# Moving the drives of 8 of 32 scans to ScalarE and TensorE, and the inner projection out of the convolution

## The chip, the cores and the metric

The kernel runs on one core of a Trainium2 chip. Five engines work side by side, each through its own queue of instructions in order: PE (TensorE, matrix multiplications and transposes), DVE (VectorE), ACT (ScalarE), POOL (GpSimd) and SP (SyncE, which here only issues DMAs). They meet through semaphores. SBUF is the memory that all of them read, PSUM the one that PE writes[...]. The metric is the device time of one execution in microseconds (us), from the first to the last instruction. Everything is fp32.

## The reference

Two layers on x of shape (2, 256, 256, 128), each as x = x + layer(group_norm(x)). The first is an attention along one axis of the image; the change doesn't touch it. The second is a selective scan over the 65,536 pixels of each image, with 256 inner channels and 16 states for each:

```python
xz = x @ in_proj_w.T
xi, z = jnp.split(xz, 2, axis=-1)
xi = silu(depthwise_conv_3x3(xi, conv_w) + conv_b)       # 256 channels
x_dbl = einsum('bdl,cd->bcl', xs, x_proj_w[0])           # xs is xi, L = H * W
dts, Bs, Cs = x_dbl[:, :8], x_dbl[:, 8:24], x_dbl[:, 24:]
delta = softplus(einsum('brl,dr->bdl', dts, dt_w[0]) + dt_b)
# for every channel d and state n, along the pixels t:
#   h = exp(delta * A) * h + (delta * xs) * Bs ;  y = sum over n of h * Cs
y = y + Ds * xs
y = layer_norm(y) * ln_g + ln_b
y = y * silu(z)
return y @ out_proj_w.T
```

(Names are shortened and the scan is put in two lines; the computation is that of the reference.)

## The kernel before

The program has two stages. The first computes group statistics and the attention, and leaves the first layer's result in DRAM as `x1`. The second walks over the two images in 128 steps of four rows, T = 1024 pixels each (`R`, `T`, `steps`).

A step has 32 scan units. A unit is a group of 32 channels with four states each, so that 32 x 4 = 128 partitions hold one recurrence each, and time runs along the free dimension. Two halves of 128 channels, four groups `m` of states and four groups `q` of channels make the 32. For a unit:

- `fetch` (line 1003) loads what it needs by DMA: `delta` and `du` = delta x xs, each row repeated for the four states, and the rows of B (`bb`) and C (`cc`), each repeated for the 32 channels. Each of these is 512 KB in SBUF. `delta_r` has five buffers, `du_r` three pairs, `bb` and `cc` two each.
- `decay` (1034): ACT takes exp(delta x A) into the PSUM tile `da`, of which there are two, for odd and even units.
- `drive` (1042): POOL multiplies du by B for two units at once into `hb`.
- `scan` (1055): DVE's tensor_tensor_scan runs h = da x h + hb from the stored state, and leaves h in `da`, or in `hb` where POOL will read it.
- `remember` (1062): ACT copies the last column of h to the state.
- `product` (1067) on DVE, or `products` (1077) for a pair on POOL: h x C into `yc`. POOL takes five pairs and a single unit of each step (`POOLED`, `SINGLE`, lines 638 and 639), DVE the other 21.
- `add_up` (1100): PE adds the four states of each channel with the 128x32 matrix `sel`. Four units write 32 rows each of the PSUM tile `y`; `y_out` copies it.

Beside the scans of step k run the pieces that prepare later steps (`project`, line 675) and finish earlier ones (`finish`, line 862). Preparation turns the image rows so that channels lie on partitions, normalises them (`xn`, with a column of padding at either side), and computes the inner projection and the 3x3 convolution in one: nine accumulated matmuls of 128x512 with weights `w_tap`, the projection's weights times one tap each (`conv`, 731). Then come the gate's projection (`gate`), two SiLUs, the projection to delta, B and C (`states`, `size`), softplus, and `times` (828), where POOL multiplies delta by xs. Results go through DRAM, so that `fetch` can repeat them. Finishing a row takes the layer norm over channels, the gate (`gated`, on DVE) and the output projection.

The order of instructions on PE, ACT, DVE and POOL is that in which the code writes them (`tc.manual_schedule`); the order on SP is the scheduler's. The loop at the end (line 1134) goes through time slots t, one for each unit, and writes for each slot the fetch for six slots ahead, the drive for three ahead, the decay for one ahead, the scan, and then whatever pieces stand in that slot's list. `at(t, piece)` puts them there; preparation starts 84 slots before the first scan of its step (`base - 12`, with base = 32 k - 72).

Stretches of lines in the text above are those of the kernel before. A function's place in the queue follows from this loop alone:

```python
if 0 <= t + 3 < end and t % 2:
    drive(t + 3)
if 0 <= t + 1 < end:
    decay(t + 1)
if 0 <= t < end:
    scan(t)
```

Of the kernel before, what the change touches and what calls it, by code (L numbers as in the profile page):

```python
# [15 lines left out]
P = 128  # L16
# [5 lines left out]
def attn_then_ssm_kernel(  # L22
# [113 lines left out]
    w_tap = const.tile([P, NH, 9, P], F32, name="w_tap")  # L136
# [17 lines left out]
    )  # L154
    with tc.tile_pool(name="prep", bufs=1) as prep, tc.tile_pool(
# [4 lines left out]
        cw = prep.tile([P, NH, 9], F32, name="cw")  # L160
        nc.sync.dma_start(out=cw, in_=conv_w.rearrange("(h p) o i j -> p h (o i j)", p=P))
# [41 lines left out]
        for h in range(NH):  # L203
            for tap in range(9):
                wt = prep2.tile([P, P], F32, name="wt")
                nc.vector.tensor_scalar(wt, inp[:, h, :], cw[:, h, tap : tap + 1], None, ALU.mult)
                transposed(w_tap[:, h, tap, :], wt, P)
            transposed(w_z[:, h, :], inp[:, NH + h, :], P)
            for i, by in enumerate((lng_c, lnb_c)):
                transposed(w_out[:, i, h, :], outp[:, h * P : (h + 1) * P], P)  # L210
                nc.vector.tensor_scalar(
                    w_out[:, i, h, :], w_out[:, i, h, :], by[:, h : h + 1], None, ALU.mult
                )
            transposed(w_xp[:, h, :], xpw[:, h * P : (h + 1) * P], 64)
            transposed(w_dt[:, h, :], dtw[:, h, :], P)
            nc.vector.tensor_scalar(d_diag[:, h, :], ident, ds_c[:, h : h + 1], None, ALU.mult)
# [415 lines left out]
    RB = TB // W  # L632
# [5 lines left out]
    POOLED = (6, 14, 22, 26, 30)  # L638
    SINGLE = 11
    s1 = ctx.enter_context(tc.tile_pool(name="s1", bufs=1))  # L640
    s2 = ctx.enter_context(tc.tile_pool(name="s2", bufs=2))
    s3 = ctx.enter_context(tc.tile_pool(name="s3", bufs=3))
    s4 = ctx.enter_context(tc.tile_pool(name="s4", bufs=4))
# [10 lines left out]
    slots = {}  # L654
    between = {}

    def at(t, piece, *args, pe=False):

        slots.setdefault(t, ([], []))[pe].append((piece, args))

    xn = s1.tile([P, R + 2, WP], F32, name="xn")
    nc.gpsimd.memset(xn, 0.0)
    given = {}
# [6 lines left out]
    for i, piece in enumerate(pieces):  # L672
        at(i - 2, piece)

    def project(k):
# [3 lines left out]
        base = k * NU - 72  # L679
# [4 lines left out]
        def bank(shape, name):  # L684

            o["n"] = o.get("n", 0) + (k == 0)
            pool, tag = ((ps_p, "p"), (ps_f, "f"))[o["n"] % 2]
# [10 lines left out]
        def begin():  # L698
            if s == 0:
                if k > 0:  # L700
                    nc.gpsimd.memset(xn[:, 0, 1 : W + 1], 0.0)
# [7 lines left out]
            else:  # L709
                nc.scalar.copy(xn[:, 0:2, 1 : W + 1], xn[:, R : R + 2, 1 : W + 1])  # L710
            if n < R:
                nc.gpsimd.memset(xn[:, 2 + n, 1 : W + 1], 0.0)
# [9 lines left out]
        def normalise(to, m):  # L722
            nc.scalar.activation(
                xn[:, to : to + m, 1 : W + 1],
# [6 lines left out]
        def conv(h, i, taps):  # L731
            if taps[0] == 0:
                o["u"] = bank([P, RB, W], "u_ps")
            for tap in taps:
                dy, dx = divmod(tap, 3)
                nc.tensor.matmul(  # L736
                    o["u"],
                    w_tap[:, h, tap, :],
                    xn[:, i * RB + dy : i * RB + dy + RB, dx : dx + W],
                    start=(tap == 0),  # L740
                    stop=(tap == 8),
                )
# [11 lines left out]
        def silu_xs():  # L754
            nc.scalar.activation(o["xs"], o["xs"], AF.Silu)
            exp_and_ln()
            v["xs"] = dr.tile([NH, P, T], F32, name="xs_d")
            nc.sync.dma_start(out=v["xs"].rearrange("h p t -> p h t"), in_=o["xs"])

        def gate(h, i):  # L760
            o["z"] = bank([P, RB, W], "z_ps")
            nc.tensor.matmul(  # L762
                o["z"],
                w_z[:, h, :],
                xn[:, 1 + i * RB : 1 + (i + 1) * RB, 1 : W + 1],
# [4 lines left out]
        def gate_out(h, i):  # L770
            if (h, i) == (0, 0):
                o["sz"] = s1.tile([P, NH, T], F32, name="sz")
            nc.scalar.copy(  # L773
                o["sz"][:, h, i * TB : (i + 1) * TB], o["z"].rearrange("p r w -> p (r w)")
            )

        def silu_z():
            nc.scalar.activation(o["sz"], o["sz"], AF.Silu)
            exp_and_ln()
            v["sz"] = dr.tile([NH, P, T], F32, name="sz_d")  # L780
            nc.sync.dma_start(out=v["sz"].rearrange("h p t -> p h t"), in_=o["sz"])
# [12 lines left out]
        def states_out(i):  # L794
            if i == 0:
                v["bc"] = dr.tile([2 * NS, T], F32, name="bc_d")
                o["xd"] = s1.tile([64, T], F32, name="xd")
# [14 lines left out]
        def size_out(h, i):  # L812
            if (h, i) == (0, 0):
                o["delta"] = s1.tile([P, NH, T], F32, name="delta")
# [20 lines left out]
        at(base - 12, load)  # L835
        at(base, begin)
        for r in range(0, n, RB):
            t = base + r // RB
            at(t, turn, "raw", r, min(RB, n - r), pe=True)
            at(t + 1, normalise, 2 + r, min(RB, n - r))  # L840
        CY = NU // 4
        for c in range(4):
            h, i = divmod(c, NB)
            t = base + c * CY + 3
            for dt, taps in ((0, (0, 1, 2)), (1, (3, 4, 5)), (2, (6, 7)), (3, (8,))):
                at(t + dt, conv, h, i, taps, pe=True)
            at(t + 5, conv_out, h, i)
        for t, (h, i) in ((2, (0, 0)), (24, (0, 1)), (25, (1, 0)), (26, (1, 1))):
            at(base + t, gate, h, i, pe=True)
            at(base + t + 1, gate_out, h, i)  # L850
        at(base + 28, silu_z)
        at(base + 36, silu_xs)
        for t, i in ((40, 0), (41, 1)):
            at(base + t, states, i, pe=True)
            at(base + t + 1, states_out, i)
        for t, (h, i) in ((42, (0, 0)), (48, (1, 0)), (49, (0, 1)), (50, (1, 1))):
            at(base + t, size, h, i, pe=True)
            at(base + t + 1, size_out, h, i)
        at(base + 52, softplus)
        at(base + 55, times)  # L860

    def finish(k):

        b, s = steps[k]
        for r in range(R):
            if k + 1 < len(steps):
                a = (r + 1) * (NU // R)
            else:
                a = 4 + r * (NU // R // 2)
            finish_row(k, b, R * s + r, r * W, (k + 1) * NU + a)  # L870

    def finish_row(k, b, row, t0, a):
# [14 lines left out]
        def fetch():  # L887
# [9 lines left out]
        def turn():  # L897
# [11 lines left out]
        def stats():  # L909
            yn = o["yn"] = room(  # L910
                "yn", "delta", lambda t: t[:, :, 0:DI], [P, WT, DI], [P, NH, T], s1
            )
# [6 lines left out]
        def scales():  # L919
# [5 lines left out]
        def norm():  # L925
# [8 lines left out]
        def back():  # L934
# [9 lines left out]
        def gated():  # L944
            o["yg"] = room("yg", "xs", lambda t: t[:, :, 0:W], [P, NH, W], [P, NH, T], s2)
            nc.vector.tensor_tensor(o["yg"], o["yd"], o["szr"], ALU.mult)  # L946

        def mix():
# [13 lines left out]
        def leave():  # L962
# [14 lines left out]
        at(a, fetch)  # L977
        for i, piece in (
            (0, turn),
            (1, stats),  # L980
            (2, scales),
            (3, norm),
            (4, back),
            (7, mix),
            (8, leave),
        ):
            at(a + i, piece, pe=piece in (turn, back, mix))
        between[a + 5] = gated
# [3 lines left out]
    units = {}  # L992

    def unit(t):

        k, i = divmod(t, NU)
        h, i = divmod(i, NM)
        m, q = divmod(i, NQ)
        return k, h, m, q
# [3 lines left out]
    def fetch(t):  # L1003
        k, h, m, q = unit(t)
        v = given[k]
        if q == 0:

            for name, row in (("bb", m * SR), ("cc", NS + m * SR)):
# [197 lines left out]
```

## Time and profile before

| what | us |
|---|---|
| median of three runs | 15813.17 (15807.9 to 15815.29) |
| span of the profiled execution | 15811.9 |
| first scan starts, last scan ends, in that execution | 2631.2, 15772.6 |
| one scan on DVE, 128x1024 | 2.34 |
| one product on DVE | 1.22 |
| one drive or product of a pair on POOL, 128x2048 | 4.54 |
| one exponential on ACT, 128x1024 | 1.12 |

The profile's page gives for each engine the busy time, its share of the span and the number of instructions. Its second part cuts the span in 40 slices, with the busy share of each in tenths. Its fifth part groups instructions by line, engine and shape; after the first bar stand the group's busy time in us and the mean of one in ns, after the second the idle time of the engine just before them and what ended it. Fp32 matmuls are recorded as two instructions each, transposes as one. Neighbouring instructions on an engine overlap a little in the record, so the sum over groups can pass the engine's busy time.

### The profile page before, as it was taken

The page shows a single profiled execution, that of the slowest core. Times are in us where ns is not written, and L with a number is a line of the kernel's source. Part 1 is how long each engine was busy: PE and PEld are TensorE (multiplying, and loading weights), DVE is VectorE, ACT ScalarE, POOL GpSimd, SP SyncE. Part 2 cuts the span into 40 slices and gives each one's busy share as a digit, 9 for nine tenths or more (in the row PEclk, how much of TensorE's full clock was granted, in tenths as well). Part 3 has the DMA queues.
Part 4 walks back from the last instruction along what each step waited for, and adds up shares of the span by engine and source line. Part 5 has one row for each costly group of instructions (what it writes and reads, how often), then busy time and mean ns, then how long its engine had stood idle before and what let it go on. Part 6 is the DMA issues. An engine that isn't in the chain of part 4 may idle for free. (4 is left out here: it accounts for less than half of the span.)

```text
span 15811.9 us, 177304 instructions
## 1 busy us (share of the span) xinstructions
PE 13767.7 (87%) x59451; PEld 6979.9 (44%) x59451; DVE 14381.3 (91%) x12134; ACT 10831.9 (69%) x20003; POOL 13322.4 (84%) x3216
## 2 busy tenths in 40 slices
PE   6999998888888888888888888888888888888887
PEld 5877884333333333333333333333333333333333
DVE  6665555999999999999999999999999999999998
ACT  4555555777777777777777677777777777777775
POOL 1111113999999999999999999999999999999998
PEclk8999998999999999999999999999999999999998
DMA  5322223777676776767677667777677777776765
GB/s 194 126 97 82 81 96 121 242 246 240 239 242 241 243 244 241 240 240 245 241 245 244 230 237 244 242 243 244 241 240 243 245 242 243 246 240 241 243 244 194
DMA packets 1426852, 3452.05 MB, mean 218 GB/s; under 512 B 117736, under 2 KB 709136, under 8 KB 1405456
## 3 DMA queue, kind: packets, MB, share of 16 engines
q1 hardware_dynamic: 1425936, 3440.72, 62.7%
q8 instruction: 467, 7.65, 0.2%
q14 instruction: 449, 3.68, 0.1%
HBM read 2752.41 MB, written 687.88 MB: 218 GB/s over the span
## 5 line engine op out<-in xcount | busy, mean ns | idle before, releaser
L1048 POOL TENSOR_TENSOR hb<-du_r,bb 128x2048 f32<-128x2048 f32 x2048 | 9247.5, 4543 | 87.8 <-DMA du_r<-du_d 16.1
L1060 DVE TENSOR_TENSOR_SCAN da<-da,state,hb 128x1024 f32<-128x1024 f32 x2688 | 6301.6, 2344 | 3.5 <-POOL state L1139 3.2
L1038 ACT ACTIVATE da<-delta_r,a_neg 128x1024 f32<-128x1024 f32 x4096 | 4581.5, 1119 | 85.1 <-DMA delta_r<-delta_d 6.0
L736 PE MATMUL u_ps<-xn,w_tap 128*128 128x512 f32 x9216 | 4237.6, 600 | 27.1 <-ACT sz L773 24.1
L1075 DVE TENSOR_TENSOR yc<-da,cc 128x1024 f32<-128x1024 f32 x2688 | 3284.5, 1222 | 253.2 <-PE y L1107 99.1
L1060 DVE TENSOR_TENSOR_SCAN hb<-da,state,hb 128x1024 f32<-128x1024 f32 x1408 | 3234.5, 2335 | 79.6 <-ACT state L1065 65.0
L1084 POOL TENSOR_TENSOR yc<-hb,cc 128x2048 f32<-128x2048 f32 x640 | 2906.8, 4542 | 86.1 <-ACT state L1065 66.4
L736 PEld LDWEIGHTS u_ps<-xn,w_tap 128*128 128x128 f32 x9216 | 1672.3, 190 | 2303.3 <-issue 1862.5
L1107 PE MATMUL y<-yc,sel 128*32 128x512 f32 x16384 | 2408.2, 712 | 20.2 <-POOL yc L1084 19.4
L458 POOL TENSOR_TENSOR x1g<-xc,bo_all 128x512 f32<-128x512 f32 x256 | 316.1, 1275 | 1844.9 <-DVE stats L513 1836.2
L1065 ACT COPY state<-da 128x1 f32<-128x1 f32 x2688 | 426.4, 159 | 1858.9 <-DVE yc L1075 1850.9
L1107 PEld LDWEIGHTS y<-yc,sel 128*32 128x32 f32 x16384 | 492.5, 126 | 1926.2 <-issue 1709.2
L762 PE MATMUL z_ps<-xn,w_z 128*128 128x512 f32 x1024 | 751.6, 825 | 625.5 <-ACT sz L773 316.9
L901 PE MATMUL yt<-centre,ys 128*128 128x256 f32 x4096 | 1030.9, 395 | 265.7 <-ACT ob L971 264.9
L408 ACT ACTIVATE e<-s_ps,nmx 128x256 f32<-128x256 f32 x1024 | 477.1, 476 | 971.8 <-DVE nmx L399 873.6
L804 PE MATMUL dt_ps<-xd,w_dt 8*128 8x512 f32 x1024 | 695.8, 764 | 507.2 <-ACT delta L815 414.1
L1065 ACT COPY state<-hb 128x1 f32<-128x1 f32 x1408 | 268.5, 191 | 1058.0 <-DVE hb L1060 1057.9
L901 PEld LDWEIGHTS yt<-centre,ys 128*128 128x128 f32 x4096 | 742.6, 191 | 445.3 <-ACT ob L971 361.5
L954 PE MATMUL o_ps<-w_out,szr 128*128 128x128 f32 x4080 | 790.0, 275 | 0.0
L954 PE MATMUL o_ps<-w_out,yg 128*128 128x128 f32 x4080 | 789.1, 275 | 0.0
L375 DVE TENSOR_TENSOR v<-v_ps,bv_all 128x512 f32<-128x512 f32 x256 | 176.9, 691 | 581.1 <-PE v_ps L368 581.1
L954 PEld LDWEIGHTS o_ps<-w_out,yg 128*128 128x128 f32 x4080 | 660.4, 192 | 26.9
(162 smaller groups left out, 17185.1 us busy)
## 6 DMA issues: line engine op xcount, KB each, us to landing
bb<-bc_d SPq DMA_DIRECT2D x1024, 512.0 KB, 4.1
cc<-bc_d SPq DMA_DIRECT2D x1024, 512.0 KB, 5.3
delta_r<-delta_d SPq DMA_DIRECT2D x1024, 512.0 KB, 6.3
du_r<-du_d SPq DMA_DIRECT2D x1024, 512.0 KB, 5.2
sz_d<-sz SPq DMA_DIRECT2D x128, 1024.0 KB, 6.5
xs_d<-xs SPq DMA_DIRECT2D x128, 1024.0 KB, 9.5
xr<-xs_d SPq DMA_DIRECT2D x256, 512.0 KB, 6.6
delta_d<-delta SPq DMA_DIRECT2D x128, 1024.0 KB, 8.8
```

Source lines behind the costliest of these rows:

```text
L736: nc.tensor.matmul(o["u"], w_tap[:, h, tap, :], xn[:, i * RB + dy : i * RB + dy + RB, dx : dx + W], start=(tap == 0), stop=(tap == 8),)
L762: nc.tensor.matmul(o["z"], w_z[:, h, :], xn[:, 1 + i * RB : 1 + (i + 1) * RB, 1 : W + 1], start=True, stop=True,)
L804: nc.tensor.matmul(o["dt"], w_dt[:, h, :], o["xd"][0:DR, i * TB : (i + 1) * TB], start=True, stop=True,)
L901: nc.tensor.matmul(o["yt"][:, j, :], ys[k, h][:, t0 + j * P : t0 + (j + 1) * P], centre[:, (1 - h) * P : (1 - h) * P + DI], start=(h == 0) ...
L954: nc.tensor.matmul(o["o"][:, j, :], o[by][:, h, j * P : (j + 1) * P], w_out[:, i, h, :], start=False, stop=(j == WT - 1 and h == NH - 1 an ...
L1038: nc.scalar.activation(da, spreads["delta", k, h, q], AF.Exp, scale=a_neg[:, g, m : m + 1])
L1048: nc.gpsimd.tensor_tensor(hb, spreads["pair", k, h, q], repeats["bb", k, h, m].unsqueeze(1).to_broadcast([P, 2, T]), ALU.mult,)
L1060: nc.vector.tensor_tensor_scan(u["h"], u["da"], u["hb"], st, ALU.mult, ALU.add)
L1065: nc.scalar.copy(st, units[t]["h"][:, T - 1 : T])
L1075: eng.tensor_tensor(u["yc"], u["h"], repeats["cc", k, h, m], ALU.mult)
L1084: nc.gpsimd.tensor_tensor(yc, hb, repeats["cc", k, h, m].unsqueeze(1).to_broadcast([P, 2, T]), ALU.mult)
L1107: nc.tensor.matmul(y[q * CQ : (q + 1) * CQ, cols], sel, units[t + q]["yc"][:, cols], start=False, stop=(m == NSG - 1),)
```

## The change

Four things change in the second stage.

First, the drives of eight of the 32 units of a step, those of the last group of states (`TURNED` = 3), no longer come from POOL. PE turns du so that time lies on partitions (`turn_du`), and B likewise (`turn_b`). With a pixel on each partition, B is one number for each partition and state, so ACT multiplies with its `scale` operand (`drives`), state by state, and writes every fourth element of `zt`. PE then turns each unit's 128 channels and states back, eight 128x128 blocks, into the PSUM tile `da` (`turn_in`). Such a unit's decay goes to SBUF instead, and its scan takes the two operands in exchanged places.

Second, the inner projection is computed by itself. `inner` makes four image rows of 32 channels at a time, each row in its own 32 partitions of the output, and ACT copies it (`inner_out`). The convolution then needs only three matmuls for each output row and group of 32 channels, one for each horizontal offset, since the three vertical taps lie on the partitions; they are 128x32 in weights and 256 columns or 255 wide. `xn` loses its padding.

Third, POOL multiplies by C for eight pairs of units instead of five and a half, in place, and DVE for 16 units instead of 21. The work tiles of drives and products are one pool of six. The order of units is another (`PAIRS`), and the rows of B and C that are repeated are loaded eleven times a step instead of 16. The state of a pooled pair is stored by one copy.

Fourth, every piece has a time of its own in a table, in slots from the start of its step; all pieces are sorted by it, and the DMAs on SP keep this order too.

The diff, cut to its core:

```diff
-    w_tap = const.tile([P, NH, 9, P], F32, name="w_tap")
+    w_in = const.tile([P, NH, P], F32, name="w_in")
+    w_cv = const.tile([P, NCG, RB, 3, CQ], F32, name="w_cv")
...
-    POOLED = (6, 14, 22, 26, 30)
-    SINGLE = 11
+    TURNED = NSG - 1
+    PAIRS = (
+        (0, 0, 0), (0, 0, 2), (0, 1, 0), (0, 1, 2), (0, 2, 0), (0, 3, 2), (0, 3, 0), (0, 2, 2),
+        (1, 2, 0), (1, 3, 2), (1, 3, 0), (1, 2, 2), (1, 1, 0), (1, 1, 2), (1, 0, 0), (1, 0, 2),
+    )
+    POOLED = (2, 4, 10, 12, 18, 20, 26, 30)
+    TIMES = {
...
+        "drives": (
+            -8.898, -8.755, 2.16, 8.854, -5.671, -4.828, -5.842, -1.931, -5.258, 3.165, -5.885,
+            6.474, 2.13, 5.925, -3.57, 1.156,
+        ),
...
+        "load": (-52.341,),
...
+        "turn_in": (9.374, 10.415, 10.881, 11.321, 17.974, 18.627, 19.701, 20.235,),
...
+    }
...
-        def conv(h, i, taps):
...
+        def inner(h, i, j, f=0):
...
+            for q in range(2):
+                c = (2 * j + q) * CQ
+                for r in range(SR):
+                    nc.tensor.matmul(
+                        o["xi", j][r * CQ : (r + 1) * CQ, q, :],
+                        w_in[:, h, c : c + CQ],
+                        xn[:, i * RB + r, :],
+                        start=True,
+                        stop=True,
+                    )
+
+        def inner_out(j):
+            nc.scalar.copy(o["xin"][:, 2 * j : 2 * j + 2, :], o.pop(("xi", j)))
+
+        def conv(h):
+            o["u"] = bank([P, RB, W], "u_ps")
+            for r in range(RB):
+                for i, (dx, a, z) in enumerate(((1, 0, W), (0, 1, W), (2, 0, W - 1))):
+                    for q in range(NQ):
+                        nc.tensor.matmul(
+                            o["u"][q * CQ : (q + 1) * CQ, r, a:z],
+                            w_cv[:, h * NQ + q, r, dx, :],
+                            o["xin"][:, q, a + dx - 1 : z + dx - 1],
+                            start=(i == 0),
+                            stop=(i == 2),
+                        )
...
+        def turn_du(i):
+            o["ut", i] = bank([P, 2, DI], "ut_ps", IN_F["turn_du"][i])
+            for j in range(2):
+                t = (2 * i + j) * P
+                for h in range(NH):
+                    nc.tensor.transpose(
+                        o["ut", i][:, j, h * P : (h + 1) * P], o["xs"][:, h, t : t + P], ident
+                    )
+
+        def turn_du_out(i):
+            if i == 0:
+                v["zt"] = s6.tile([P, T // P, DI, SR], F32, name="zt")
+            nc.scalar.copy(v["zt"][:, 2 * i : 2 * i + 2, :, SR - 1], o["ut", i])
+
+        def drives(j, n, m):
+            for r in range(n, m):
+                nc.scalar.activation(
+                    v["zt"][:, j, :, r],
+                    v["zt"][:, j, :, SR - 1],
+                    AF.Copy,
+                    scale=v["bt"][:, j, r : r + 1],
+                )
...
+    def turn_in(t):
+
+        k, h, m, q = unit(t)
+        da = units[t]["da"] = ps_d.tile([P, T], F32, name=f"da{t % 2}")
+        a = h * P + q * CQ
+        for j in range(T // P):
+            nc.tensor.transpose(
+                da[:, j * P : (j + 1) * P],
+                given[k]["zt"][:, j, a : a + CQ, :].rearrange("p c r -> p (c r)"),
+                ident,
+            )
...
-        nc.vector.tensor_tensor_scan(u["h"], u["da"], u["hb"], st, ALU.mult, ALU.add)
+        ins = ("hb", "da") if turned(t) else ("da", "hb")
+        nc.vector.tensor_tensor_scan(u["h"], u[ins[0]], u[ins[1]], st, ALU.mult, ALU.add)
...
+        if not pooled(t):
+            nc.scalar.copy(st[:, g, m : m + 1], units[t]["h"][:, T - 1 : T])
+        elif t % 2:
+            nc.scalar.copy(st[:, g - 1 : g + 1, m], units[t]["pair"][:, :, T - 1])
...
-        for t in range(min(slots), max(slots) + 1):
...
+        for _, _, piece, args in sorted(events, key=lambda e: e[:2]):
+            piece(*args)
```

## The prediction

> **What bounds the kernel now.** I read the page's busy line, then its slices, then the costliest groups, then a table of 1000 us from the middle, and last the waits and timelines there.
>
> ```profile
> PE 13767.7 (87%) x59451; PEld 6979.9 (44%) x59451; DVE 14381.3 (91%) x12134; ACT 10831.9 (69%) x20003; POOL 13322.4 (84%) x3216
> ...
> POOL 1111113999999999999999999999999999999998
> ...
> L1048 POOL TENSOR_TENSOR hb<-du_r,bb 128x2048 f32<-128x2048 f32 x2048 | 9247.5, 4543 | 87.8 <-DMA du_r<-du_d 16.1
> ...
> L1075 DVE TENSOR_TENSOR yc<-da,cc 128x1024 f32<-128x1024 f32 x2688 | 3284.5, 1222 | 253.2 <-PE y L1107 99.1
> ...
> L1084 POOL TENSOR_TENSOR yc<-hb,cc 128x2048 f32<-128x2048 f32 x640 | 2906.8, 4542 | 86.1 <-ACT state L1065 66.4
> ```
>
> The slices show two programs: attention in the first sixth, where POOL is idle, then 128 equal scan steps. The averages of the first line hide that. The middle shows the second stage alone (columns as in its head):
>
> ```profile
> core 0: us, PE busy (x) PEld busy (x) DVE busy (x) ACT busy (x) POOL busy (x), PEclk, DMA share, GB/s
> 9000.00:10000.00 1000.00, 864.00 (x3484) 385.37 (x3483) 968.38 (x553) 709.57 (x1238) 979.82 (x224) 0.92 0.69 237
> ```
>
> POOL is busy 98% and DVE 97%; PE 86%, ACT 71%. The timeline has the first scan at 2631.2 us and the last ending at 15772.6, so a step takes 13141.4/128 = 102.67 us, and 15811.9 - 13141.4 = 2670.5 us lie outside. POOL's groups, divided by 128, give 72.2 (16 drives) + 22.7 (5 pair products) + 2.4 (the single product) + 4.5 (L831) = 101.9 us. DVE's give 74.5 (32 scans) + 25.7 (21 products) + 2.7 (4 gates) = 102.9, less some 3 us by which neighbours overlap. Two engines are full at once; a change must unload both.
>
> ACT is 29% idle, mostly harmlessly: it waits for results that arrive in DVE's rhythm.
>
> ```profile
> ACT state L1065 <- DVE yc L1075: 1850.9, 1870, 4.9
> ...
> ACT state L1065 <- DVE hb L1060: 1057.9, 1033, 2.1
> ...
> ACT ob L971 <- PE o_ps L954: 458.9, 475, 4.2
> ```
>
> The third line (3.6 us a step) is of another kind: in-order ACT stands behind a PE result. This must shrink when ACT is filled.
>
> **What the Trainium skill says.** "SBUF — State Buffer", section SBUF: two separate sides, says a DVE operation with two SBUF inputs and a GpSimd operation lock each other out. Here DVE always has one operand in PSUM, and its scans take the same 2335 to 2344 ns beside a full POOL: agreed. The changed scans keep one operand in PSUM too. The same page's note on cachelines (section Door 1) says that accesses which each reach a new 16-byte line are penalised; the new drives read and write fp32 at a stride of four, which is that. No run here shows an ACT operation at such a stride. "ScalarE: Activation LUTs", What ACT_TABLE_LOAD costs, gives 1283 ns per load (trace: 1283) and 0.833 ns per element (trace: (1912 - 1119)/1024 = 0.77 between its sizes). "TensorE: Matmul & The Clock Gate", Back-to-back issue gap, puts pairs of weight load and matmul at about 81 ns for 128 columns; the trace never shows less than 110.
>
> **The change, per step.** A step keeps 32 scans.
>
> POOL: 16 drives become 12, products become 8 pairs, the single one goes. 12 x 4.515 + 8 x 4.542 + 4.55 = 95.1 us: -6.8.
>
> DVE: 21 products become 16: -5 x 1.222 = -6.1. From its unoverlapped 99.9 this leaves 93.8.
>
> ACT has these rows for the price of what it gains:
>
> ```profile
> L927 ACT ACTIVATE yn<-yt,rstd 128x256 f32<-128x256 f32 x1020 | 418.0, 460 | 0.1
> ...
> L773 ACT COPY sz<-z_ps 128x512 f32<-128x512 f32 x512 | 297.0, 580 | 50.4 <-PE z_ps L762 48.0
> ```
>
> 32 activations of 128x256 in `drives`: 418.0/1020 = 0.41 each, 13.1. Copies from PSUM of 128x512: 8 in `inner_out`, 4 in `turn_du_out`, 12 x 0.58 = 7.0; `turn_b_out` 0.3. The joined SiLUs save two table loads, 2.6. `remember` goes from 32 to 24 and saves 1.4. Net +16.4 on 71.0 x 1.0267 = 72.9: 89.3. If every strided access took twice its element time, drives add 32 x 0.213 = 6.8 and the four copies 1.7 (0.833 ns by the skill, an estimate): 97.8. It cannot be cheaper than contiguous. I take the low end for the likeliest case: both ends lie under the old 102.7, but only the low one under POOL.
>
> PE, from these rows:
>
> ```profile
> L736 PE MATMUL u_ps<-xn,w_tap 128*128 128x512 f32 x9216 | 4237.6, 600 | 27.1 <-ACT sz L773 24.1
> ...
> L1107 PE MATMUL y<-yc,sel 128*32 128x512 f32 x16384 | 2408.2, 712 | 20.2 <-POOL yc L1084 19.4
> ...
> L938 PE MATMUL yd<-ident,yn 128*128 128x128 f32 x2040 | 309.1, 275 | 26.3 <-ACT yn L927 25.6 <-ACT ob L971 0.5
> ```
>
> The convolution's 72 instructions at 0.46 = 33.1 us go (a fp32 matmul is recorded as two; a transpose as one). In come 64 `inner` and 96 `conv` matmuls of 32 output rows and 256 columns, 320 instructions. Their shape is that of `y`, four of which run side by side: 0.147 each for 512 columns, so 0.0735 for 256, 23.5 us. Its best bursts, 1.92 us for 16, would give 19.2; if a narrow one cost as much as a wide one, it is 38 to 47. Transposes: 64 `turn_in`, 16 `turn_du`, 8 `turn_b`, 88 x 0.1515 = 13.3. Sum: 864/1000 x 102.67 = 88.7 - 33.1 + 23.5 + 13.3 = 92.4, in which isolated matmuls count with their tails.
>
> DMA: the repeated rows fall from 16 to 11 transfers of 512 KB, and the queue stands at 0.69; nothing is won, since no engine waits for them. SP's instructions are now in the hand-made order too: a load that waits for its buffer holds all behind it. `fetch_delta` is the nearest such case, with eight loads through five buffers; the built order gives each a buffer whose last reader stands earlier in ACT's order, so I cost it at 0 to 1 us.
>
> New waits: a turned scan waits for eight transposes on PE, which wait for all `drives` on ACT. Behind them on PE queue the sums and the projection; behind a late one DVE waits. `da` has two buffers, so a transposed drive must be made within the preceding scan: 2.35 us for about 0.9 of transposes and 0.6 of latency. PE has some 1.85 us of `add_up` in between twice, so it just misses at times; I allow 1 us a step. The same slack applies to `decay`: 2.35 us against 1.12 + 0.19.
>
> So: POOL 95.1, DVE 93.8, PE 92.4, ACT 89.3. Before, the fullest engine lost 102.67 - 101.9 = 0.8 us a step. With four in-order engines between 89 and 95, I allow 2.4: 97.5 us.
>
> Outside the steps: the first load stands 52 slots before its scans instead of 84, so less of the next steps' projection precedes the first scan. PE ran convolutions of three steps from 2521 to 2629 before it; I take 25 us off (0 to 50). Preparation has 18 small transposes fewer and five tiny loads more, beside the statistics: nothing, 5 us either way. The tail of 39 us stays.
>
> Sum: 2670.5 - 25 + 128 x 97.5 = 15125.5. The profiled execution is 1.3 us under the median of the runs, 15813.2: no correction.
>
> **The rivals.**
> A (0.50), as above: steps of 96.5 to 99, 15000 to 15320.
>
> B (0.27): the stride doubles the element time and ACT becomes the bound. 97.8 + 2.4 of losses = 100.2: 2645.5 + 128 x 100.2 = 15471. For it: the skill's note. Against: ACT alone was never limited in the trace, so nothing confirms it. Sign: `drives` near 0.65 us each and DVE waiting for ACT.
>
> C (0.18), the slower side: narrow matmuls don't get cheaper with fewer columns, and PE becomes the bound. At the burst rate of `y`, 1.92 us for 16 instructions, 320 cost 38.4, and PE needs 88.7 - 33.1 + 38.4 + 13.3 = 107.3: 2645.5 + 128 x 107.3 = 16380. It decides from (102.7 - 68.9)/320 = 0.106 us each. For it: no 128-wide instruction in the trace starts less than 0.11 after another. Against: those have full weights to load, and the skill's 81 ns would give 25.9 us.
>
> D (0.05): the fixed order locks the engines well and less is lost, with the prologue at its best: 95.8 a step, 2620 + 12262 = 14882.
>
> **How the numbers follow.** The time is A's, 15125. Low 14870 takes in D; high 15780 takes in B with more loss, and leaves out C. What a measurement of this kernel can tell from no change is about 0.2%, 32 us. Faster: A, B and D less 0.03 for B landing near the old step: 0.79; same 0.03; slower 0.18. A's own range stands above.
>
> **What would show it.** Scans 32 apart some 97.5 us apart; POOL again near 98% with 21 instructions a step; products on DVE 2048 in all; `drives` at 0.41 against 0.65; `inner` and `conv` together near 23 us a step. It is wrong if PE is above 98%, or if DVE's idle time before turned scans exceeds 3 us a step.

## The result and the profile after

The changed kernel takes 16276.49 us (median of four runs, 16262.75 to 16279.14) against 15811.76 in the same session: a ratio of 1.0293, 95% interval 1.0279 to 1.0308. It is slower by 2.9%; the prediction was 15125.

The profiled execution has a span of 16261.0 us. The first scan starts at 2602.1 and the last ends at 16219.3, so a step takes 106.4 us where 97.5 were forecast and 102.67 were before, and 2644 us lie outside the steps, where 2645.5 were forecast. All of the miss is in the step.

From the page of the changed kernel: busy times, ACT's slices, and groups of instructions:

```profile
PE 13681.8 (84%) x102443; PEld 8025.9 (49%) x102443; DVE 13663.5 (84%) x11479; ACT 13899.9 (85%) x24467; POOL 12670.3 (78%) x2960
...
ACT  3555557999999999999999999999999999999997
...
L976 ACT ACTIVATE zt<-zt,bt 128x256 f32<-128x256 f32 x4096 | 3073.1, 787 | 37.6
...
L851 PE MATMUL u_ps<-raw,w_cv 128*32 128x255 f32 (+1 forms) x24576 | 1819.8, 456 | 896.3 <-ACT raw L844 337.4
...
L835 PE MATMUL xi_ps<-xn,w_in 128*32 128x256 f32 x16384 | 1164.9, 392 | 342.9 <-ACT raw L844 325.9
```

ACT, at 69% of the span before, now stands at nine tenths or more in every slice but those in which the scans begin and end. L976 is `drives`: 3073.1/4096 = 0.75 us of busy time each, 24.0 us a step. (The 787 ns in the line is the mean length of one; neighbours overlap a little, so the busy time is less.) Groups on PE are read by the busy time, since many narrow matmuls run side by side and the mean of one says nothing of the cost: (1819.8 + 1164.9)/128 = 23.3 us a step for `conv` and `inner`.

The middle of the changed kernel, 1000 us, in the columns PE, PEld, DVE, ACT, POOL, clock, DMA share, GB/s:

```profile
9000.00:10000.00 1000.00, 823.90 (x6487) 444.41 (x6486) 886.82 (x489) 913.60 (x1530) 905.71 (x201) 0.93 0.60 210
```

Times 106.4, that is ACT 97.2 us a step, POOL 96.4, DVE 94.4, PE 87.7. No engine is full: the fullest idles 9.2 us a step, where the fullest of before idled 0.8. The chain that ended last, which the page follows back from the last instruction, spends most of its time on ACT all the same:

```profile
ACT 44%; PE 24%; DVE 8%; issue 5%; DMA 1%; POOL 1%; SPq 0%; POOLq 0%; DVEq 0%; ACTq 0%
```

The waits of the changed kernel (total us, times, longest):

```profile
DVE work L1275 <- ACT da L1237: 469.7, 436, 2.8
...
POOL work L1297 <- ACT state L1284: 432.9, 154, 7.8
POOL work L1244 <- DVE da L1275: 409.9, 133, 4.5
...
DVE work L1292 <- DMA cc<-bc_d: 171.2, 114, 5.3
```

Before, ACT waited for DVE. Now DVE waits for decays from ACT, and POOL for copies of the state by ACT and for a buffer that DVE has not read. The last line is small here, 1.3 us a step, and turned out to be a second cause in waiting.

One step of the changed kernel, cut where ACT begins and ceases to wait for PE (same columns):

```profile
9000.00:9024.00 24.00, 19.07 (x156) 10.23 (x155) 21.91 (x13) 23.53 (x37) 20.92 (x6) 1.00 0.68 237
9024.00:9047.00 23.00, 22.22 (x117) 12.10 (x116) 19.90 (x12) 17.52 (x31) 20.66 (x5) 0.85 0.60 209
9047.00:9106.40 59.40, 46.84 (x430) 25.48 (x429) 52.90 (x30) 56.98 (x98) 55.24 (x13) 0.91 0.55 198
```

ACT is busy 98%, 76% and 96% of these stretches (97, 78 and 95% over twenty steps). The first and last hold the drives and the copies for them, which have to be done between the turn of du and the first turned scan. In the 23 us between, ACT stands behind PE results (`dt`, `ob`, `yt`), PE being 97% busy there (95% over twenty steps). So the average of 91% is one stretch near its limit and another that can't take any of its work.

### The profile page after: what moved, and what is told of

Same layout as the page of the kernel before. It is cut to its first block, busy times and chain, and to the rows that moved or that the text cites. A ratio compares the mean times of both kernels' runs of the same rounds, so it can differ in the third digit from the quotient of the medians.

```text
span 16261.0 us, 265160 instructions
## 1 busy us (share of the span) xinstructions
PE 13681.8 (84%) x102443; PEld 8025.9 (49%) x102443; DVE 13663.5 (84%) x11479; ACT 13899.9 (85%) x24467; POOL 12670.3 (78%) x2960
## 4 chain that ended last, share of the span: by engine, by line
ACT 44%; PE 24%; DVE 8%; issue 5%; DMA 1%; POOL 1%; SPq 0%; POOLq 0%; DVEq 0%; ACTq 0%
ACT zt L976 14%; ACT da L1237 10%; DVE work L1275 7%; PE y L1325 5%; PE u_ps L851 4%; PE dt_ps L916 4%; ACT work L1237 3%; ACT raw L844 3%; ACT zt L972 3%; PE o_ps L1104 2%; PE da L1263 2%; PE xi_ps L835 2%; ACT sz L891 2%; PE yt L1053 2%; PE xd_ps L898 1%
## 5 line engine op out<-in xcount | busy, mean ns | idle before, releaser
L1244 POOL TENSOR_TENSOR work<-du_r,bb 128x2048 f32<-128x2048 f32 x1536 | 7163.3, 4679 | 793.6 <-DVE da L1275 409.9
L1275 DVE TENSOR_TENSOR_SCAN da<-da,state,work 128x1024 f32<-128x1024 f32 x2048 | 4776.2, 2344 | 256.2 <-ACT da L1237 216.9
L1237 ACT ACTIVATE da<-delta_r,a_neg 128x1024 f32<-128x1024 f32 x3072 | 3430.6, 1119 | 82.0 <-DVE work L1275 47.4
L976 ACT ACTIVATE zt<-zt,bt 128x256 f32<-128x256 f32 x4096 | 3073.1, 787 | 37.6
L1292 DVE TENSOR_TENSOR work<-da,cc 128x1024 f32<-128x1024 f32 x2048 | 2465.1, 1219 | 495.7 <-ACT state L1282 261.4
L1275 DVE TENSOR_TENSOR_SCAN work<-da,state,work 128x1024 f32<-128x1024 f32 x1024 | 2388.8, 2343 | 478.8 <-ACT da L1237 469.7
L1297 POOL TENSOR_TENSOR work<-work,cc 128x2048 f32<-128x2048 f32 x512 | 2350.9, 4592 | 419.0 <-ACT state L1284 415.0
L851 PE MATMUL u_ps<-raw,w_cv 128*32 128x255 f32 (+1 forms) x24576 | 1819.8, 456 | 896.3 <-ACT raw L844 337.4
L1275 DVE TENSOR_TENSOR_SCAN work<-work,state,da 128x1024 f32<-128x1024 f32 x1024 | 2346.4, 2333 | 158.0 <-PE da L1263 132.6
L1297 POOL TENSOR_TENSOR work<-work,ccx 128x2048 f32<-128x2048 f32 x512 | 2318.3, 4552 | 19.1 <-ACT state L1284 17.8
L1325 PE MATMUL y<-work,sel 128*32 128x512 f32 x16384 | 2204.0, 641 | 15.0 <-POOL work L1297 15.0
L835 PE MATMUL xi_ps<-xn,w_in 128*32 128x256 f32 x16384 | 1164.9, 392 | 342.9 <-ACT raw L844 325.9
L1237 ACT ACTIVATE work<-delta_r,a_neg 128x1024 f32<-128x1024 f32 x1024 | 1163.4, 1148 | 2.0 <-PE y L1325 0.3
```

The costliest lines, as they stand in the source:

```text
L835: nc.tensor.matmul(o["xi", j][r * CQ : (r + 1) * CQ, q, :], w_in[:, h, c : c + CQ], xn[:, i * RB + r, :], start=True, stop=True,)
L851: nc.tensor.matmul(o["u"][q * CQ : (q + 1) * CQ, r, a:z], w_cv[:, h * NQ + q, r, dx, :], o["xin"][:, q, a + dx - 1 : z + dx - 1], start=(i ...
L976: nc.scalar.activation(v["zt"][:, j, :, r], v["zt"][:, j, :, SR - 1], AF.Copy, scale=v["bt"][:, j, r : r + 1],)
L1237: nc.scalar.activation(da, spreads["delta", k, h, q], AF.Exp, scale=a_neg[:, g, m : m + 1])
L1244: nc.gpsimd.tensor_tensor(open_pair(t, time_of(k, "drive", DRIVEN.index(t % NU))), spreads["du", k, h, q], repeat_of("bb", t).unsqueeze(1) ...
L1275: nc.vector.tensor_tensor_scan(u["h"], u[ins[0]], u[ins[1]], st, ALU.mult, ALU.add)
```

## The experiments

Steps below are (span - 2644)/128. The theory at the start: the strided access of `drives` costs too much on ACT (S). Its rival: the order written for SP makes loads late (Q).

**Contiguous drives by another order of partitions (e1).** States outside, channels inside, everywhere: the drives touch runs of 32 floats.

```diff
-v["zt"] = s6.tile([P, T // P, DI, SR], F32, name="zt")
+v["zt"] = s6.tile([P, T // P, NCG, SR, CQ], F32, name="zt")
...
-            .unsqueeze(1)
-            .to_broadcast([CQ, SR, T]),
+            .unsqueeze(0)
+            .to_broadcast([SR, CQ, T]),
```

> The states of a unit are put outermost on the partitions everywhere (state, channel instead of channel, state), so that the drives on ScalarE read and write runs of 32 neighbouring elements instead of every fourth. The order of all pieces stays. Theory 1 (the stride of 16 bytes makes ScalarE the bound): a drive falls from 0.79 to about 0.46 us, turn_du_out from 1.07 to 0.58; ScalarE gives up about 13 us a step, and the step falls from 106.4 to 97 to 99 us, so about 15100 to 15300 us. Theory 2 (the fixed order loses its time in waits for TensorE, the stride matters little): the drives fall likewise, but the step stays above 103 us, over 15830 us.

Measured: 25305.3 us, ratio 1.6004 (1.5977 to 1.6031). Every expectation missed, since the loads became slow: the middle moves 126 GB/s instead of 210, and DVE, ACT and POOL wait for `cc`, `delta_r` and `du_r`. The cost of the instruction can still be read, in the groups of e1:

```profile
L979 ACT ACTIVATE zt<-zt,bt 128x256 f32<-128x256 f32 x4096 | 1936.5, 503 | 37.8
```

0.473 us busy each against 0.75: by the groups, the stride costs 32 x 0.28 = 9 us a step, and the four copies of L972, at 570 ns instead of 1075, another 2. ACT's whole busy time falls by less, from 97.2 to 89 us a step (500.8 of 1000 us, at 177.1 a step), since neighbours overlap in part.

**No drives at all (e2).**

```diff
-            for r in range(n, m):
+            for r in range(n, m)[0:0]:
```

> Leaves out the 32 multiplications of drives on ScalarE (turn_du_out, turn_b and turn_in stay), so the turned units get unscaled or old data. ScalarE gives up 24 us a step. Theory 1: VectorE and GpSimd become the bound, the step is 95.5 to 98 us, 14870 to 15190 us; and no less, since GpSimd's sum is 95.1. Theory 2: above 103 us a step, since the waits for TensorE in the stretch before the drives stay.

Measured: 15949.86 us (one execution), a step of 103.9. ACT falls to 76 us of load and the kernel is still slower than the one before: S is not all. The number is that of theory 2, the reason is not, for what holds the step is a load. The waits of e2 show what stands there:

```profile
DVE work L1292 <- DMA cc<-bc_d: 705.4, 126, 8.3
```

5.5 us a step, nearly always one long wait. In the changed kernel one such wait looks like this on DVE's timeline (start, duration, idle before):

```profile
9186.45 1.22 DVE L1292 TENSOR_TENSOR work<-da,cc 128x1024 f32<-128x1024 f32 x1 [5.29 <-DMA cc<-bc_d]
```

and SP's timeline, here of the step before that one, shows the queue in which that load stands:

```profile
9066.78 1.16 SPq L1155 DMA_DIRECT2D du_r<-du_d  x2
9068.04 0.54 SPq L1306 DMA_DIRECT2D xr<-xs_d  x1
9068.62 0.51 SPq L1152 DMA_DIRECT2D bb<-bc_d  x1
9069.17 0.61 SPq L1152 DMA_DIRECT2D cc<-bc_d  x1
```

The last C load of a step is due at 28.034 and stands behind loads of du due at 26.08, which wait until POOL's drives have freed a pair of `du_r`. By the table of times, the buffer that C wants is free since the product at 23.505.

**Which side of the stride costs (e3, e4).** e3 reads contiguous data of another tile and writes with stride; e4 reads with stride and writes a contiguous block.

```diff
 e3
-                    v["zt"][:, j, :, SR - 1],
+                    o["xs"][:, 0, 0:DI],
 e4
-                    v["zt"][:, j, :, r],
+                    v["zt"][:, (j + 1) % (T // P)].rearrange("p d r -> p (d r)")[:, r * DI : (r + 1) * DI],
```

> The drives write every fourth element as before, but read 256 neighbouring elements of another tile (other data, so other results). If the stride costs on the reading side, a drive takes about 0.46 us and the time is that of e1_runs_of_32; if on the writing side, 0.79 us and 16270 us as in the changed kernel; if on both by halves, about 0.6 us and 15500 to 15900 us.

> The drives read every fourth element as before, but write 256 neighbouring elements (into the next block, so other results). The mirror of e3_write_strided: 0.79 us if reading costs, 0.46 us if writing does, about 0.6 us if both do by halves.

Measured: 15884.55 and 16131.17 us (one execution each). The group of e3, then that of e4:

```profile
L976 ACT ACTIVATE zt<-xs,bt 128x256 f32<-128x256 f32 x4096 | 2571.8, 761 | 0.0
```

```profile
L976 ACT ACTIVATE zt<-zt,bt 128x256 f32<-128x256 f32 x4096 | 2951.2, 779 | 8.5
```

By the length of one, a single strided side costs nearly what two do (787); runs of 32 take 503. Busy time, which is what fills ACT, differs more: 0.63 with a strided write, 0.72 with a strided read, 0.75 with both, 0.47 with neither. So the reading side is the dearer one, and e3 comes out between the extremes that were expected. The time follows in order: 20.1 us of drives, 103.4 a step; 23.1 and 105.4; 24.0 and 106.4.

**The C load ahead of du, alone and without drives (e5, e6).**

```diff
-        "fetch_c": (-2.23, 2.972, 5.721, 10.592, 28.034,),
+        "fetch_c": (-2.23, 2.972, 5.721, 10.592, 23.9,),
```

> One number is changed: the last of the five C loads of a step is due at 23.9 instead of 28.034, so on SP it stands ahead of the du loads due at 26.08 instead of behind them (its buffer's last reader is the product due at 23.505). Theory Q (SP's written order is a second bound: the C rows are late because a du load ahead of them waits for POOL): the waits of VectorE's products for the C rows go from 1.3 us a step towards nothing, and since ScalarE is the larger bound in this kernel, 0.5 to 1.5 us a step come off: 16080 to 16210 us. Theory S (ScalarE's strided drives alone set the time): 16240 to 16280 us. Rival: the earlier C load stands in the way of others on SP, and du arrives later: over 16300 us.

> The drives of the turned units are left out as in the run without them (their 32 multiplications on ScalarE; the output is not the reference's), and the last C load is moved ahead of the du loads as well. Theory Q: the wait for C, 5.6 us a step in the run without drives, goes, and with ScalarE at 76 us of load a step POOL and VectorE bound at 95 to 99 us: 14950 to 15400 us. If the C wait was only a symptom of something else that is late (du, or the scans that hand POOL its buffers), the time stays within 0.7% of the 15950 us of that run.

Measured: e5 16284.26 us, ratio to the kernel before 1.0297 (1.0282 to 1.0313), no change from the changed kernel; e6 15467.48, ratio 0.9782 (0.9767 to 0.9796), 482 us below e2. In e5 the wait for C is gone and the time with it is not: DVE's wait for decays grows from 469.7 to 551.4 us instead, so ACT was the later one anyway. In e6, where ACT has 77 us of load, the move pays 3.7 us a step, which leaves 15467 just above the range of theory Q (15400 at most). The waits of e6:

```profile
POOL work L1244 <- DVE da L1275: 224.0, 133, 4.0
POOL work L1244 <- DMA du_r<-du_d: 167.4, 126, 3.0
DVE work L1292 <- DMA cc<-bc_d: 126.8, 99, 2.9
```

What is left is POOL: busy 959 of 1000, 96.1 of 100.2 us, losing 1.75 a step to buffers that DVE still reads and 1.3 to du; 1.0 a step of DVE's wait for C remains.

**Contiguous reads, with and without the C load (e7, e9).** The copy of the turned du goes back into `xs`, whose columns have just been turned and are dead once du has left by DMA; drives read that and write with stride. e7 has the C load at 23.9, e9 at 28.034.

```diff
-            nc.scalar.copy(v["zt"][:, 2 * i : 2 * i + 2, :, SR - 1], o["ut", i])
+            nc.scalar.copy(o["xs"][:, :, i * DI : (i + 1) * DI], o["ut", i])
...
-                    v["zt"][:, j, :, SR - 1],
+                    o["xs"][:, j % 2, j // 2 * DI : (j // 2 + 1) * DI],
```

> The computation is whole. The copy out of the turned du (L972) goes into the tile it was turned from, in contiguous runs, and the drives read that and write with stride; the C load stands ahead of du as well. ScalarE loses 8 strided copies' excess (4 x (1.07-0.57) = 2 us) and 32 x 0.12 us = 4 us of the drives: 97.1 to 91 us a step. Theory S+Q (the sum of both bounds): 99 to 101.5 us a step, 15320 to 15640 us. Theory S alone: as with the run that writes with stride, 15800 to 15900 us. Rival: the copy waits for the transfer of du out of the same tile, ScalarE stands in order behind it, and the gain is lost: over 16000 us.

> The fourth corner of the square: the drives read in contiguous runs as in e7, and the last C load stays at 28.034 as in the changed kernel. If the two causes hide each other (each pays only once the other is gone): ScalarE is relieved by 6 us a step, the wait for C takes over, and the time is near the run that wrote with stride, 15780 to 15900 us. If the C load matters only without drives: 15530 to 15580 us, as e7. If the two simply add: as the C load alone moved nothing, again 15530 to 15580 us.

Measured: e7 15549.37 us, ratio 0.9836 (0.9819 to 0.9852): 1.6% faster than the kernel before. e9 15821.05, ratio 1.0012 (1.0003 to 1.0021). The waits of e9, and of e7:

```profile
DVE work L1292 <- DMA cc<-bc_d: 403.6, 118, 5.8
```

```profile
DVE work L1292 <- DMA cc<-bc_d: 4.5, 7, 1.3
```

The square is complete: neither 16276, C load alone 16284, contiguous reads alone 15821, both 15549. The C load is worth nothing while ACT is late and 272 us once it isn't. e9 falls in the range of the first case, but the two do not hide each other: relieving ACT pays 455 us by itself.

**SP's order given back to the scheduler (e8).** `SP` is taken out of `engines` of the second part; nothing else moves.

> SP is taken out of the written order of the second part: its DMAs are placed by the scheduler as in the kernel before; all other engines keep their instructions and order. Theory Q: the waits for C, du and delta shrink, and the time falls to what ScalarE's 97 us with its own waits allows, 103 to 105 us a step: 15830 to 16090 us. Theory S: 16200 to 16300 us. Rival: the written order is better than the scheduler's, which now also starts loads late: over 16350 us.

Measured: 16836.05 us, ratio 1.0652 (1.0636 to 1.0668). Q in its broad form is refuted: the written order is better than the scheduler's by 560 us, and one entry of it was shown to be bad. POOL's drives now idle 702.4 us for "issue", nothing that the profile shows; what holds them stays open.

**Two microseconds off ACT where it waits (e10).** e5 with a square in place of the softplus, so without its two table loads of 1.28 us, at 19.08 of 32.

```diff
-            nc.scalar.activation(o["delta"], o["delta"], AF.Softplus)
-            exp_and_ln()
+            nc.scalar.activation(o["delta"], o["delta"], AF.Square)
+            None
```

> Of e5 (whose ScalarE load and time are those of the changed kernel), the softplus is replaced by a square, which leaves out its two table loads of 1.28 us each (the output is not the reference's). They stand at 19.08 of 32, in the stretch where ScalarE waits for TensorE and has idle time. Theory L (ScalarE bounds only the stretches with drives, and its load can't be spread over the step): no change or less than 0.6 us a step, 16200 to 16300 us. Theory U (any microsecond of ScalarE counts, its 9 us idle a step are losses spread evenly): 2.56 us a step less, 15930 to 15990 us.

Measured: 16273.02 us (16269.02 to 16291.36), against 16265.23 to 16286.42 for e5: no change. The waits of e10:

```profile
ACT ob L1121 <- PE o_ps L1104: 619.9, 309, 6.1
```

It was 304.7 in e5: (619.9 - 304.7)/128 = 2.5 us a step, all that was taken out, has become waiting for PE. In e7 some 5.8 us are taken out where the drives stand, and the step is 5.7 shorter than in e5. So a microsecond of ACT counts where the drives stand and not between.

One other thing differs between these runs, the clock that TensorE was granted as a share of full speed, of e5 first and then of e7:

```profile
core 0: 16284.6 us, clock 0.925
core 0: 15552.3 us, clock 0.961
```

It is 0.924 to 0.926 in every execution of e5 and e10 and 0.959 to 0.964 in those of e7, so it goes with the kernel. From the 10th scan of a step to its 24th, where no drive stands and PE is busiest, e5 takes 42.8 us at a clock of 0.91, e10 42.4 at 0.91 and e7 40.8 at 0.96 (means over 90 steps); the other 18 scans take 63.9, 63.9 and 60.1. So about two of e7's 5.9 us by this count lie in the stretch that PE holds, at the higher clock. The clock is higher in every run that only took work off ACT where the drives stand (0.931 in e4, 0.956 to 0.967 in e2, e3, e6 and e9); why, no run here shows. It has no part in the difference between the kernels before and after, whose clocks are 0.925 and 0.926.

**The turn of du later (e11).** In e7 the first copy waits 183.4 us in all for the du transfer out of `xs`. Turn, copy and the first two drives move 0.8 of a slot.

```diff
-            -8.898, -8.755, 2.16, 8.854, -5.671, -4.828, -5.842, -1.931, -5.258, 3.165, -5.885,
+            -8.1, -8.0, 2.16, 8.854, -5.671, -4.828, -5.842, -1.931, -5.258, 3.165, -5.885,
...
-        "turn_du": (-9.691, -6.021, -7.213, -4.676,),
-        "turn_du_out": (-9.002, -5.843, -7.087, -4.562,),
+        "turn_du": (-8.9, -6.021, -7.213, -4.676,),
+        "turn_du_out": (-8.2, -5.843, -7.087, -4.562,),
```

> e7 with the first copy out of the turned du 0.8 of a slot later (and its turn and its first two drives with it), so that it no longer waits 1.4 us a step on ScalarE for the transfer of du out of the same tile. If ScalarE still bounds there: up to 1.4 us a step less, 15370 to 15540 us. If POOL and VectorE bound by now: 15530 to 15580 us. If the drives, now later, hold up others: over 15600 us.

Measured: 15776.64 us, ratio 0.9979 (0.9972 to 0.9987), 227 us worse than e7. DVE's two waits for decays (L1275 on L1237), 158.7 and 131.1 us in e7, are now:

```profile
DVE da L1275 <- ACT da L1237: 277.2, 262, 2.2
...
DVE work L1275 <- ACT da L1237: 247.8, 271, 1.6
```

Up 235 us. The copy's wait for the transfer is gone (4.1 us in all), but the later drives hold up decays, as the last line of the expectation had it; ACT's stretch with the drives has little room even in e7.

**What slowed e1 (e12, e15, e16).** e12 is the changed kernel with only the source order of the delta and du loads of e1. e15 is e1 with every repeated load cut into four of 32 partitions, and e16 the same with C at 23.9.

```diff
 e15, e16
+        for r in range(SR):
+            nc.sync.dma_start(
+                out=tl[r * CQ : (r + 1) * CQ, :],
+                in_=given[k]["bc"][a + r, :].partition_broadcast(CQ),
+            )
```

> Of e1's two changed orders of rows, only that of the spreads of delta and du is made (the 32 rows four times over, instead of each row four times in a row); the repeats of B and C stay as in the changed kernel, and so does all else (the rows of delta and du no longer fit those of B and C: the output is not the reference's). If the order of rows in the spreads is what slowed e1: above 21000 us, with VectorE, ScalarE and POOL waiting for delta and du. If the repeats of B and C did it (one row to 32 neighbouring partitions): 16200 to 16400 us. If both share it: in between, 17500 to 21000 us.

> e1 again (every repeat and the drives in the order state, channel; drives and copies in runs of 32), but each repeated load is written as four of 32 partitions and 128 KB, so that no load has an outermost dimension of four. If the outermost four was what slowed e1: loads land as fast as in the changed kernel, ScalarE's drives cost 0.47 busy and its step 97 - 32 x 0.27 - 4 x 0.5 = 86 us; the C load still stands late on SP, so the wait for C takes over as in the run without drives and in e9: 15750 to 15980 us. If it was the order of rows in memory or on the partitions as such: over 20000 us. If SP, with four times as many loads to issue at 0.5 to 0.6 us each, becomes the bound: 16300 us and more.

> The same with the last C load at 23.9. If the price of the stride and the C load are the two causes and nothing else is: as the run without drives and with the C load moved, 15420 to 15560 us, and not the 15125 of the prediction, since POOL with 96 us loses 4 to 5 us a step there too. If the prediction's small losses (2.4 us a step) hold once ScalarE has slack: 15050 to 15250 us. If the many loads on SP cost time: over 15700 us.

Measured: e12 22799.86 us (one execution), with 143 GB/s in the middle; e15 16996.95, ratio 1.0751 (1.0735 to 1.0767); e16 16584.94, ratio 1.0491 (1.0474 to 1.0509). The delta and du loads alone make most of e1's excess. The Trainium skill, "DMA: Bandwidth & Descriptors", Rules for kernel authors, says that an outermost dimension of fewer than 16 confines a DMA to at most that many engines, and e1's loads have a leading repeat of four. The rates agree (126 GB/s with it, 199 and 203 in e15 and e16, in the same order of rows); which engines worked, no run here shows. The drives cost 504 ns in both and ACT has slack at 88 us a step. SP, which issues the loads, is not full: its instructions fill 51 and 52% of the same 1000 us. But four times as many loads keep the DMA engines at 0.76 and 0.78 for fewer GB/s than the changed kernel moves at 0.60, and delta and C are late (DVE waits 1237 and 848 us for C). So neither reached the time of e6.

**Runs of two floats (e17).** The order on partitions is (pair, state, channel of the pair); loads are cut in two, each with an outermost dimension of 16; C at 23.9.

```diff
-v["zt"] = s6.tile([P, T // P, DI, SR], F32, name="zt")
+v["zt"] = s6.tile([P, T // P, DI // 2, SR, 2], F32, name="zt")
```

> The computation is whole. Channels go in pairs: the order on the partitions is (pair of channels, state, channel of the pair), so the drives and the copies of the turned du touch runs of two floats (8 bytes) at a stride of 32 bytes; each repeated load is two of 64 partitions and 256 KB with an outermost dimension of 16; the last C load is at 23.9. If two floats in a run are enough to bring back the contiguous price (0.50 us for 128x256, 0.57 for the copy), ScalarE has some 86 us a step, and with the loads no slower than before the time is that of the run without drives and C moved, 15420 to 15600 us. If a run of two costs as much as single floats (0.79 us): 16200 us and more. In between (0.6 to 0.7 us): 15500 to 15900 us. If twice as many loads make C and delta late, as four times as many did: 15800 to 16400 us at the contiguous price.

Measured: 16169.9 us, ratio 1.0232 (1.0214 to 1.0249); the loads were late, as the last line allowed (DVE waits 562.7 us for C). But the groups of e17 settle the price:

```profile
L980 ACT ACTIVATE zt<-zt,bt 128x256 f32<-128x256 f32 x4096 | 2057.5, 535 | 37.6
```

535 ns with pairs at a stride of 32 bytes, against 787 with single floats at 16 and 504 in runs of 32.

## Why the prediction was wrong

The step that failed first is the choice in ACT's part, "I take the low end for the likeliest case". It took 0.41 for a drive and 0.58 for a copy; they are 0.75 and 1.07, and ACT's load is 97.2 us a step for 89.3. The sum itself was sound for drives without the stride: e15, with runs of 32, has ACT at 88. The reason given, that only the low end lies under POOL, says how the cases differ, not which is true. The only evidence on the stride was the skill's note on cachelines ("SBUF — State Buffer", Door 1), and that spoke for the high end. The runs agree with it: single floats cost 787 ns, two neighbours to a line 535 (e17). That this made the kernel slow is shown by e9, which only takes the stride off the drives' reads and off the copies before them: 15821 us, so 455 of the 465 us between the two kernels are gone.

Rival B priced that load well, 97.8, and its sign came true: dear drives, and DVE waiting for ACT. Its second term failed: "97.8 + 2.4 of losses", where the loss is 9.2. Loads were compared as averages over a step. The drives have a window, and within it ACT had hardly any slack, while the stretch between was held by PE (e10 against e7). The fullest engine of each of the three stretches, over twenty steps, adds up to 23.3 + 21.8 + 56.4 = 101.5 us, 4 more than the fullest engine of the whole step; the other 5 are waits within the stretches. The two signs of being wrong that the prediction named did not come (PE above 98%: it was 82%; DVE idle over 3 us before turned scans: 1.2), since both watched PE.

The cost of SP's order, "0 to 1 us", was right for the changed kernel by accident (e5: nothing). The load named as nearest, delta, was not the one: C was, behind du. The late C load costs 272 us with ACT relieved and 482 without drives.

The losses of case A, 2.4, were too small by themselves. With no drives at all and C nearly in time, e6 takes 100.2 us a step beside a POOL of 96.1: 4.1 lost. So A's 97.5 would hardly have come even at the contiguous price; no run here has contiguous drives and loads in time together. Of the 8.9 us that the step misses, 2.7 are this (one of them POOL's own load, 96.1 for 95.1). The other 6.2 come with the drives and the late C load; e7, which only writes with stride, wins 5.6 of them back.

What held: POOL 95.1 (96.4), DVE 93.8 (94.4); `inner` with `conv` 23.5 (23.3), which removes rival C, the slower case that was foreseen; one microsecond of waiting for turned drives, 1.2 measured (158.0 us before these scans, in 128 steps); the 25 us off the prologue, 29 measured. PE as a whole was put too high, 92.4 for 87.7. C had the direction right and the mechanism wrong: the kernel is slower through ACT, not PE. Two readings were off without consequence: the 0.77 ns per element lies between an activation with a scale for each partition and others without one, so it is no price of an element; and the shortest step between matmuls of 128 columns in the trace is 108 ns, not 110.

e7 keeps the change, takes one of the two strided sides away and moves one load. It is faster than both kernels.

## What to carry to other kernels

Before moving work to the idlest engine, cut the step where the new work may run and add up each engine's load within that window; an average (71% here, 91% with the new work) hides a window that the new work fills. If moved work turns a layout round, don't let both the reads and the writes of an operation be strided, or keep two fp32 neighbours together, and look at what that asks of the loads. When a fix changes nothing, keep it and try it again once the other bound is gone: of two things that are late, the later one hides what the other costs (e5 against e7).

## What was not expected of the hardware

For single floats at a stride of 16 bytes, an ACT instruction of 128x256 is nearly as long with one strided side as with two: 761 ns (write), 779 (read), 787 (both), 503 (runs of 32). Its busy time in a row of them tells the sides apart: 0.63, 0.72, 0.75 and 0.47 us. A copy of 128x512 from PSUM into a tile strided like this takes 1075 ns, and 570 into runs of 32.

The order of the dimensions of the repeating loads decided how fast they came: with each row four times in a row, the kernel moves 210 GB/s in its middle, where ACT bounds it; with the 32 rows four times over, for delta and du alone, it moves 143 and waits for them (e12).

Cutting 512 KB loads in two (e17) made each half land hardly sooner: 6.5, 6.0, 6.1 and 4.1 us from issue to landing (medians, for delta, du, B and C), where whole ones took 6.2, 6.3, 6.8 and 4.7. The DMA engines were busy 0.74 instead of 0.60 for the same 210 GB/s.
